# Weights in tiles of sixteen pairs, three sets of split parts, field 0 in an output slot: a bilinear pair kernel on one core

## The chip, the core and the metric

The kernel runs on one core of one Trainium2 chip. The metric is device time in microseconds. The core has five engines that run side by side and meet at semaphores: TensorE (PE; matrix products into PSUM), VectorE (DVE), ScalarE (ACT), GpSimd (POOL) and SyncE (SP), which here only issues DMAs. Sixteen DMA engines move data between the chip's main memory and the core's SBUF; SP, ACT and POOL each feed them from a queue of their own.

## The reference

There are 32 fields, each a batch of 1024 vectors of 128 numbers, and 496 pairs (i, j) of fields with i < j. Each pair has its own 128 x 128 matrix. For each pair the kernel multiplies the batch of field i by the matrix, and then, element by element, by field j:

```python
v_i = inputs[:, I_IDX, :]                              # (1024, 496, 128)
v_j = inputs[:, J_IDX, :]
transformed = jnp.einsum('bpd,ped->bpe', v_i, W)       # W: (496, 128, 128)
return transformed * v_j
```

All is float32. The output has 1024 x 496 x 128 numbers, 260 MB; the weights have 32.5 MB, the fields 16.8 MB.

## The kernel before

**Order.** Pairs are worked in the order i = 30, 29, ... 0, and for each i all j > i; a pair's number q is its place in this order. A field lies transposed, 128 x 1024. The main loop (L300) counts half pairs u: each step issues the first products of half u (`first`, L257) and the rest of half u - 3 (`second`, L273). The program fixes the order of the instructions on every engine; no planner moves them.

**Products.** The first 15 pairs are multiplied directly in float32 (L265). All others use TensorE's faster float32r format: weights and fields are each split in three parts, and a half pair is made of three 512-column matmuls: xh,wh and xl,wl (L268), then, after ACT has scaled PSUM in place (L270), xd,wd (L279). When both halves stand, one VectorE multiplication (L244) takes PSUM and field j and writes 128 x 1024 numbers into an output tile. PSUM holds four pairs.

**Splitting.** `split_w` (L144) splits a chunk of two pairs: ACT makes wh (L149), POOL makes wl (L151) and wd (L152, L153). There are four sets of these parts, so chunk c waits for the last use of chunk c - 4; its split is issued right behind that use. `split_x` (L161) splits half a field: ACT makes xh (L167), POOL makes xl (L168, L169), VectorE xd some steps later (L334). One split, of weights or of a field, is issued every second half step, the one that is needed soonest first.

**Weights.** Raw weights come in tiles of eight pairs: 128 rows of 4 KB, 62 loads of 512 KB, in three buffers. Loads up to tile 11 have places in the loop (`w_at`), later ones follow when the last split of an older tile has been issued (`ring`). Most are one DMA from SP (L132). The 25 loads in `WAPART` are divided (`load_apart`): POOL loads 112 rows over 14 of the 16 DMA engines, SP the last 16 rows, one on each engine. POOL's queue goes round the engines with a pointer; a tiny transfer (`move_on`, L111) puts the pointer back, so that the same two engines are left out each time. Field 0 comes late into one of the three weight buffers, in its turn in `ring`.

**Output.** The first 292 pairs are stored in groups of four, one DMA of 2 MB in 16 KB rows; the others in groups of three, 1.5 MB in 12 KB rows; ACT issues them (L318). A group's tile is four of the twelve slots of one buffer (`slots`), or one of the tiles g3, g2, g1, g0, which serve as output tiles until four fields each are loaded into them (the places in `XAT`, less `OWAIT`). From pair 292 on the twelve slots alone are used, four groups of three in turn. VectorE can write a slot only when the store that read it has landed.

Of the kernel before, what the change touches and what calls it, by code (L numbers as in the profile page):

```python
# [7 lines left out]
F32 = mybir.dt.float32  # L8
F32R = mybir.dt.float32r
ALU = mybir.AluOpType  # L10

P = 128
NF = 32
NQ = NF * (NF - 1) // 2
BT = 1024
HB = 512
WC = 2
WL = 8
OG = 4
EPS = 2.0**-12  # L20
NATIVE = 5
# [2 lines left out]
LAG = 3  # L24
SPREAD = 18
PB = 4
WB = 3
WLEAD = 12
XAFTER = 54
WRING = 12  # L30
XLEAD = 5

XG = 4
NE = 14
ROWS = 8 * NE
WAPART = tuple(range(12, 62, 2))
BACK = 3
FOURS = 73
NS = 12
XAT = (313, 219, 141, 52)  # L40
OWAIT = 20
XSTEP = 6
SLAG = 2
# [7 lines left out]

def _groups():

    return [(q, OG) for q in range(0, OG * FOURS, OG)] + [(q, OG - 1) for q in range(OG * FOURS, NQ, OG - 1)]


@with_exitstack
def kernel(
# [22 lines left out]
    nc = tc.nc  # L81
# [3 lines left out]
    xpool = ctx.enter_context(tc.tile_pool(name="x", bufs=1))  # L85
    spool = ctx.enter_context(tc.tile_pool(name="xs", bufs=2))
    rpool = ctx.enter_context(tc.tile_pool(name="wr", bufs=WB))
    wpool = ctx.enter_context(tc.tile_pool(name="ws", bufs=1))
# [5 lines left out]
    def load_x(f, pieces=1, eng=None):  # L94
        if f == 0:

            t = rpool.tile([P, WL, P], F32, tag="w", name="x_0").rearrange("p q e -> p (q e)")
        else:
            t = xpool.tile([P, BT], F32, tag=f"x{f}", name=f"x_{f}")
        s = BT // pieces  # L100
        for k in range(pieces):
            (eng or nc.sync).dma_start(out=t[:, k * s : (k + 1) * s], in_=xt[f, :, k * s : (k + 1) * s])
        x_sb[f] = t

    w_raw = {}
# [3 lines left out]
    def move_on(k):  # L109

        nc.gpsimd.dma_start(out=mark[: 2 * k], in_=xt[0, : 2 * k, :16].rearrange("(b a) n -> a b n", a=k))  # L111

    def load_apart(dst, src):
        nc.gpsimd.dma_start(out=dst[:ROWS], in_=src[:ROWS].rearrange("(b a) m n -> a b m n", a=NE))
        nc.sync.dma_start(out=dst[ROWS:], in_=src[ROWS:])
# [3 lines left out]
    def load_group(k, m):  # L119
        if m == XG - 1:  # L120
            group[k] = xpool.tile([P, XG, BT], F32, tag=f"g{k}", name=f"x_g{k}")
        f = XG * k + 1 + m
        x_sb[f] = group[k][:, m, :]
        nc.sync.dma_start(out=x_sb[f], in_=xt[f])

    def load_w(c, splits=(0, WL), eng=nc.sync):
        w_raw[c] = rpool.tile([P, WL, P], F32, tag="w", name=f"w_{c}")
        if c in WAPART:
            load_apart(w_raw[c], wt[c])
            return  # L130
        for a, b in zip(splits, splits[1:]):
            eng.dma_start(out=w_raw[c][:, a:b, :], in_=wt[c, :, a:b, :])  # L132

    scaled, taken, halved = {}, {}, {}

    def apart(inst, other, reason="the halves of a pair lie in two banks"):

        if other is not None:
            tc.declare_no_dep(inst.ins, other.ins, reason=reason)

    w_s, spent = {}, []
    w_t = [[wpool.tile([P, WC * P], F32R, tag=f"{t}{k}", name=f"{t}_{k}") for t in ("wh", "wl", "wd")] for k in range(4)]

    def split_w(c, u):  # L144

        k = c * WC % WL
        raw = w_raw[c * WC // WL][:, k : k + WC, :].rearrange("p q e -> p (q e)")
        h, l, d = w_t[c % 4]
        halved[c] = nc.scalar.mul(h, raw, 1.0 - 2.0**-13)  # L149
        apart(halved[c], halved.get(c - 4), "one engine writes both, in order")  # L150
        nc.gpsimd.tensor_tensor(l, raw, h.bitcast(F32), ALU.subtract)  # L151
        nc.gpsimd.tensor_scalar(d, h.bitcast(F32), EPS, 1.0, ALU.mult, ALU.mult)  # L152
        nc.gpsimd.tensor_tensor(d, l.bitcast(F32), d.bitcast(F32), ALU.subtract)  # L153
        w_s[c] = (h, l, d)
        if (c + 1) * WC % WL == 0:
            spent.append(c * WC // WL)

    x_s = {}
    later = []
# [1 line left out]
    def split_x(f, a, u):  # L161

        if a == 0:
            x_s[f] = [spool.tile([P, BT], F32R, tag=t, name=f"{t}_{f}") for t in ("xh", "xl", "xd")]
        s = slice(a, a + HB)
        h, l, d = [t[:, s] for t in x_s[f]]
        nc.scalar.mul(h, x_sb[f][:, s], 1.0 - 2.0**-13)  # L167
        nc.gpsimd.tensor_tensor(l, x_sb[f][:, s], h.bitcast(F32), ALU.subtract)  # L168
        nc.gpsimd.tensor_scalar(l, l.bitcast(F32), 1.0 / EPS, 1.0, ALU.mult, ALU.mult)  # L169
        if f == 0 and a > 0:  # L170
            spent.append("x")
        if f > NF - 2 - NATIVE - SHARED:
            later.append((min(u + XDLAG, 2 * first_q[f] + LAG - 1), d, h.bitcast(F32), l.bitcast(F32)))
        else:
            nc.gpsimd.tensor_tensor(d, h.bitcast(F32), l.bitcast(F32), ALU.subtract)

    nq0 = NATIVE * (NATIVE + 1) // 2
    c0 = nq0 // WC
# [2 lines left out]


    todo = []
    for c in range(c0, nchunk):
        todo.append(((c - 3) * WC + 1, max(c * WC, nq0), lambda u, c=c: split_w(c, u)))
    for i in range(NF - 2 - NATIVE, -1, -1):
        for a in range(0, BT, HB):
            at = first_q[i + 1] + 1 if i < NF - 3 - NATIVE else 2
            if 0 < i < SPREAD:
                at += (NF - 2 - i) * (2 + 3 * (a > 0)) // 10  # L190
            todo.append((at, first_q[i], lambda u, i=i, a=a: split_x(i, a, u)))
    todo.sort(key=lambda t: t[1])

    load_w(0, (0, 1, WL), nc.sync)
    load_x(NF - 2, pieces=2, eng=nc.scalar)
    load_x(NF - 1, pieces=2, eng=nc.scalar)
    load_x(NF - 3)
    load_x(NF - 4)
    load_w(1, eng=nc.sync)
    for f in range(NF - 5, NF - 4 - XLEAD, -1):  # L200
        load_x(f)
    load_w(2, eng=nc.sync)


    w_at = {}
    for c in range(WB, -(-NQ // WL)):
        free = (c - WB + 1) * WL if (c - WB) * WL < nq0 else 0
        if c < WRING:
            w_at[max(c * WL - 3 * WC + 1 - WLEAD, free)] = c

    back = []
    last = NQ // WL
    ring = [*range(WRING - WB, XAFTER + 1), "x", *range(XAFTER + 1, last)]

    ngroup = NF // XG // 2
    group_at = {q + XSTEP * (XG - 1 - m): (k, m) for k, q in enumerate(XAT) for m in range(XG)}
    assert all(q + 5 < first_q[XG * k + m + 2] for q, (k, m) in group_at.items())
    until = {f"g{k}": q - OWAIT for k, q in enumerate(XAT)}
    groups = _groups()
    group_of = {q + k: (g, k) for g, (q, n) in enumerate(groups) for k in range(n)}  # L220
    used = {t: n - 9 for n, t in enumerate(("s0", "s1", "s2", *sorted(until, reverse=True)))}

    slots = opool.tile([P, NS, BT], F32, tag="slots", name="slots")
    written = {}

    def out_tile(g):
        q, n = groups[g]
        if n < OG:
            a = (g - FOURS) * n % NS
        else:  # L230
            t = min((t for t in used if q + n <= until.get(t, NQ)), key=used.get)
            used[t] = g
            if t in until:
                return xpool.tile([P, OG, BT], F32, tag=t, name=f"ot_{g}"), None
            a = OG * int(t[1:])
        return slots[:, a : a + n, :], a
# [63 lines left out]
    for u in range(2 * NQ + LAG + SLAG):  # L300
        q = u // 2
        if u < 2 * NQ:
            i, j = pairs[q]
            if u % 2 == 0 and j == i + 1 and XG * ngroup < i - 2 - XLEAD:
                load_x(i - 2 - XLEAD)
            first(u)
            if u == 2 * nq0:
                move_on(5)
            if u % 2 == 0 and q in group_at:
                load_group(*group_at[q])  # L310
            if u % 2 == 1 and q in w_at:
                load_w(w_at[q])
            if u % 2 == 0 and q in back:
                move_on(16 - NE if max(w_raw) < WAPART[-1] else 13)
        if LAG <= u < 2 * NQ + LAG:
            second(u - LAG)
        while stores and stores[0][0] <= u - LAG:
            nc.scalar.dma_start(*stores.pop(0)[1:])  # L318
        if u % 2 == 1:
            ready = [t for t in todo if t[0] <= q]  # L320
            if ready:
                ready[0][2](u)
                todo.remove(ready[0])
        if ring[WB:] and ring[0] in spent:
            ring.pop(0)
            c = ring[WB - 1]
            if c == "x":
                load_x(0)
            else:
                load_w(c)  # L330
            if c in WAPART:
                back.append(q + BACK)
        while later and later[0][0] <= u:
            nc.vector.tensor_tensor(*later.pop(0)[1:], ALU.subtract)  # L334
# [32 lines left out]
```

## Time and profile before

| | |
|---|---|
| median of three runs | 748.13 us (743.98 to 750.29) |
| profiled execution | 741.81 us, span 739.9 us |
| moved by DMA | 310.02 MB, mean 419 GB/s |
| TensorE, ACT, VectorE, POOL busy | 703.9, 634.0, 637.3, 595.0 us |
| weight loads | SP: 36 of 512 KB, 26 of 64 KB, one of 448 KB; POOL: 25 of 448 KB |
| a store of 2 MB in `slots` | 16.5 us from issue to landing (median); of 1.5 MB 12.6 us |

A row of busy time by stage gives the stretch in microseconds, its length, then for PE, PEld (weight loads of TensorE), DVE, ACT and POOL the busy time with the number of instructions, then the granted TensorE clock (1.00 is full), the DMA engines' busy share and GB/s. A row of waits names the engine, tile and line that waited, then what ended the wait: total us, number, longest. A row of the timeline gives start, duration, engine, line, operation, and tiles as out<-in. In the summary, DMA digits are the busy share of 40 equal slices in tenths; a queue's row gives packets, MB and the share of the span of sixteen engines.

### The profile page before, as it was taken

The numbers are of one execution on the slowest core, as the hardware profiler recorded it, in microseconds if no ns is written. First come the engines' busy times: TensorE is split into PE (matmuls) and PEld (weight loads), VectorE is DVE, ScalarE is ACT, GpSimd is POOL, SyncE is SP. The second block draws the span as 40 slices with busy tenths as digits, with TensorE's granted clock in tenths as the row PEclk, the third lists the DMA queues.
The fourth block names the chain that finished last, engine by engine and source line by source line (L and its number), as shares of the span: only waits on it lengthen the run. The fifth ranks groups of instructions, "written<-read, shape, count | busy, mean of one in ns | idle before, by whom it ended". The sixth has DMA issues, their size and how long they took to land.

```text
span 739.9 us, 10346 instructions
## 1 busy us (share of the span) xinstructions
PE 703.9 (95%) x2946; PEld 550.4 (74%) x2946; DVE 637.3 (86%) x550; ACT 634.0 (86%) x1256; POOL 595.0 (80%) x882
## 2 busy tenths in 40 slices
PE   7999999999999999999899979999999999999994
PEld 3577777878778888776688758886778887777782
DVE  3898999999999999988798868987999988997884
ACT  1298999999999999998899968998989999898892
POOL 1789999999999999987789776988787888797660
PEclk9999999999999999999999999999999999999997
DMA  9999999999999999999999999999999999999998
GB/s 346 422 429 423 430 413 429 426 418 428 423 421 428 421 426 424 427 418 426 425 427 424 428 425 406 419 424 425 424 425 419 423 421 421 426 416 424 423 430 330
DMA packets 36968, 310.02 MB, mean 419 GB/s; under 512 B 5552, under 2 KB 5680, under 8 KB 19120
## 3 DMA queue, kind: packets, MB, share of 16 engines
q10 hardware_dynamic: 21888, 261.11, 83.6%
q1 hardware_dynamic: 10592, 36.77, 12.4%
q0 software_dynamic: 4432, 11.48, 4.0%
q8 instruction: 24, 0.39, 0.2%
q14 instruction: 32, 0.26, 0.1%
HBM read 49.29 MB, written 260.05 MB: 418 GB/s over the span
## 4 chain that ended last, share of the span: by engine, by line
PE 60%; DMA 22%; DVE 8%; POOL 3%; ACT 3%; issue 2%; ACTq 0%; DVEq 0%; POOLq 0%
PE po L268 38%; DMA out_dram<-slots 20%; PE po L279 18%; DVE slots L244 5%; PE po L265 4%; ACT po L270 2%; DVE xd L334 2%; DMA out_dram<-ot 1%; DVE ot L244 1%; POOL wd L153 1%; POOL wl L151 1%; POOL xl L168 1%; DMA x<-in_xt_dram 1%; POOL xl L169 0%; POOL wd L152 0%
## 5 line engine op out<-in xcount | busy, mean ns | idle before, releaser
L270 ACT ACTIVATE po<-po 128x512 f32<-128x512 f32 x962 | 553.3, 584 | 74.0 <-PE po L268 57.4
L268 PE MATMUL po<-xh,wh 128*128 128x512 f32 x962 | 382.0, 397 | 17.3 <-DVE slots L244 15.2
L279 PE MATMUL po<-xd,wd 128*128 128x512 f32 x962 | 376.4, 391 | 4.8 <-DVE xd L334 2.4
L268 PE MATMUL po<-xl,wl 128*128 128x512 f32 x962 | 377.2, 392 | 1.2 <-POOL wl L151 0.9
L244 DVE TENSOR_TENSOR slots<-po,x 128x1024 f32<-128x1024 f32 (+1 forms) x263 | 314.0, 1213 | 56.3 <-DMA out_dram<-slots 21.1
L268 PEld LDWEIGHTS po<-xh,wh 128*128 128x128 f32 x962 | 181.2, 188 | 74.0 <-DVE slots L244 30.8
L151 POOL TENSOR_TENSOR wl<-w,wh 128x256 fp32r<-128x256 f32 x241 | 184.8, 767 | 63.6 <-ACT wh L149 57.9
L279 PEld LDWEIGHTS po<-xd,wd 128*128 128x128 f32 x962 | 181.2, 188 | 45.0 <-DVE slots L244 3.2
L268 PEld LDWEIGHTS po<-xl,wl 128*128 128x128 f32 x962 | 181.3, 189 | 40.7 <-POOL wl L151 3.9
L153 POOL TENSOR_TENSOR wd<-wl,wd 128x256 fp32r<-128x256 f32 x241 | 180.3, 748 | 20.1
L244 DVE TENSOR_TENSOR slots<-po,x_g 128x1024 f32<-128x1024 f32 x123 | 148.4, 1223 | 22.3 <-DMA out_dram<-slots 8.5
L244 DVE TENSOR_TENSOR ot<-po,x 128x1024 f32<-128x1024 f32 x99 | 119.4, 1221 | 13.6 <-PE po L279 2.6
L152 POOL TENSOR_SCALAR wd<-wh 128x256 fp32r<-128x256 f32 x241 | 103.5, 429 | 20.5
L149 ACT ACTIVATE wh<-w 128x256 fp32r<-128x256 f32 x241 | 98.6, 410 | 5.7 <-DVE slots L244 5.7
L334 DVE TENSOR_TENSOR xd<-xh,xl 128x512 fp32r<-128x512 f32 x52 | 48.0, 924 | 0.0
L168 POOL TENSOR_TENSOR xl<-x_g,xh 128x512 fp32r<-128x512 f32 x32 | 41.6, 1300 | 2.2 <-ACT xh L167 2.0
L168 POOL TENSOR_TENSOR xl<-x,xh 128x512 fp32r<-128x512 f32 x20 | 25.8, 1292 | 15.8 <-ACT xh L167 15.6
L169 POOL TENSOR_SCALAR xl<-xl 128x512 fp32r<-128x512 f32 x52 | 34.4, 662 | 4.6
L265 PE MATMUL po<-x,w 128*128 128x512 f32 x60 | 29.5, 650 | 4.1 <-DMA x<-in_xt_dram 4.1
L265 PEld LDWEIGHTS po<-x,w 128*128 128x128 f32 x60 | 12.1, 207 | 20.7 <-issue 14.5
L167 ACT ACTIVATE xh<-x 128x512 fp32r<-128x512 f32 x20 | 12.3, 624 | 11.5 <-DMA x<-in_xt_dram 11.4
L167 ACT ACTIVATE xh<-x_g 128x512 fp32r<-128x512 f32 x32 | 20.0, 624 | 0.0
(8 smaller groups left out, 49.5 us busy)
## 6 DMA issues: line engine op xcount, KB each, us to landing
out_dram<-slots ACTq DMA_DIRECT2D x67, 1536.0 KB, 12.6
out_dram<-slots ACTq DMA_DIRECT2D x44, 2048.0 KB, 16.5
out_dram<-ot ACTq DMA_DIRECT2D x28, 2048.0 KB, 12.7
w<-in_wt_dram SPq DMA_DIRECT2D x36, 512.0 KB, 10.9
w<-in_wt_dram POOLq DMA_DIRECT2D x25, 448.0 KB, 11.6
x_g<-in_xt_dram SPq DMA_DIRECT2D x16, 512.0 KB, 16.3
x<-in_xt_dram SPq DMA_DIRECT2D x14, 512.0 KB, 9.4
out_dram<-slots ACTq DMA_DIRECT2D x5, 512.0 KB, 8.9
```

Source lines behind the costliest of these rows:

```text
L149: halved[c] = nc.scalar.mul(h, raw, 1.0 - 2.0**-13)
L151: nc.gpsimd.tensor_tensor(l, raw, h.bitcast(F32), ALU.subtract)
L152: nc.gpsimd.tensor_scalar(d, h.bitcast(F32), EPS, 1.0, ALU.mult, ALU.mult)
L153: nc.gpsimd.tensor_tensor(d, l.bitcast(F32), d.bitcast(F32), ALU.subtract)
L168: nc.gpsimd.tensor_tensor(l, x_sb[f][:, s], h.bitcast(F32), ALU.subtract)
L169: nc.gpsimd.tensor_scalar(l, l.bitcast(F32), 1.0 / EPS, 1.0, ALU.mult, ALU.mult)
L244: i = nc.vector.tensor_tensor(ot[:, k, s], p, f, ALU.mult)
L265: nc.tensor.matmul(po[q][:, s], w_raw[q // WL][:, q % WL, :], x_sb[i][:, s], start=True, stop=True)
L268: m = nc.tensor.matmul(po[q][:, s], w_s[c][t][:, r], x_s[i][t][:, s], start=t == 0, stop=t == 1)
L270: scaled[u] = nc.scalar.mul(po[q][:, s], po[q][:, s], 1.0 + EPS)
L279: m = nc.tensor.matmul(po[q][:, s], w_s[q // WC][2][:, r], x_s[i][2][:, s], start=False, stop=True, skip_group_check=True)
L334: nc.vector.tensor_tensor(*later.pop(0)[1:], ALU.subtract)
```

## The change

- Weight tiles hold sixteen pairs (`WL = 16`): rows of 8 KB, 31 loads of 1 MB, two buffers. The first tile comes in three pieces, the second whole before the loop. All later loads follow when the last split of the tile two before has been issued, none before pair 15.
- 13 of the 31 loads are divided over 14 engines and the rest (`WAPART`), every second one from tile 6 on, as before every second one from tile 12 of eight pairs.
- The fourth set of split weights lies in tile g0 and is used up to pair 178 only; after that there are three sets, and a split waits for the chunk three before. g0 becomes an output tile from pair 188 on.
- Field 0 is loaded at pair 432 into slot 11 of the output slots and split at pairs 444 and 448 (before: 436 and 437). For two rounds the last group has two pairs, so that slot 11 stays free.
- Fields of the four groups are loaded at pairs 308, 212, 117 and 52 (before: 313, 219, 141, 52).

```diff
-WL = 8
+WL = 16
-WB = 3
-WLEAD = 12
-XAFTER = 54
-WRING = 12
+WB = 2
+WSETS = 4
+WMORE = 178
+XZERO = 432
+XSPLIT = 444
+XROUND = 11
-WAPART = tuple(range(12, 62, 2))
+WAPART = tuple(range(6, 31, 2))
-XAT = (313, 219, 141, 52)
+XAT = (308, 212, 117, 52)
...
 def _groups():
-    return [(q, OG) for q in range(0, OG * FOURS, OG)] + [(q, OG - 1) for q in range(OG * FOURS, NQ, OG - 1)]
+    groups, q = [(q, OG) for q in range(0, OG * FOURS, OG)], OG * FOURS
+    while q < NQ:
+        k, n = divmod(len(groups) - FOURS, NS // (OG - 1))
+        n = OG - 1 - (n == NS // (OG - 1) - 1 and k - XROUND in (0, 1))
+        groups.append((q, min(n, NQ - q)))
+        q += n
+    return groups
...
         if f == 0:
-            t = rpool.tile([P, WL, P], F32, tag="w", name="x_0").rearrange("p q e -> p (q e)")
+            t = slots[:, NS - 1, :]
+            for h in (0, 1):
+                written.pop((NS - 1, h))
...
-    w_t = [[wpool.tile(...) for t in ("wh", "wl", "wd")] for k in range(4)]
+    w_t = [[wpool.tile(...) for t in ("wh", "wl", "wd")] for k in range(WSETS - 1)]
+    more = xpool.tile([P, OG * BT], F32R, tag="g0", name="w_more")
+    w_t.append([more[:, k * WC * P : (k + 1) * WC * P] for k in range(3)])
...
-        h, l, d = w_t[c % 4]
+        h, l, d = w_t[set_of[c]]
...
-        if (c + 1) * WC % WL == 0:
-            spent.append(c * WC // WL)
+        if (c + 1) * WC % WL == 0 and c * WC // WL + WB < NQ // WL:
+            ring.append(c * WC // WL + WB)
...
+    set_of, user, order = {}, {}, list(range(WSETS))
+    last_of = dict.fromkeys(order, c0 - WSETS)
     for c in range(c0, nchunk):
-        todo.append(((c - 3) * WC + 1, max(c * WC, nq0), lambda u, c=c: split_w(c, u)))
+        if c * WC == WMORE:
+            order.remove(WSETS - 1)
+        order.append(order.pop(0))
+        set_of[c] = order[-1]
+        user[c], last_of[order[-1]] = last_of[order[-1]], c
+        todo.append(((user[c] + 1) * WC + 1, max(c * WC, nq0), lambda u, c=c: split_w(c, u)))
...
             at = first_q[i + 1] + 1 if i < NF - 3 - NATIVE else 2
+            if i == 0:
+                at = XSPLIT + 4 * (a > 0)
...
-    load_w(0, (0, 1, WL), nc.sync)
+    load_w(0, (0, 1, WL // 2), nc.sync)
...
-    load_w(1, eng=nc.sync)
+    load_w(0, (WL // 2, WL), nc.sync)
     for f in range(NF - 5, NF - 4 - XLEAD, -1):
         load_x(f)
-    load_w(2, eng=nc.sync)
+    load_w(1)
...
-            t = min((t for t in used if q + n <= until.get(t, NQ)), key=used.get)
+            t = min((t for t in used if q + n <= until.get(t, NQ) and (t != "g0" or q >= WMORE + OWAIT // 2)), key=used.get)
...
-            if u % 2 == 1 and q in w_at:
-                load_w(w_at[q])
+            if u == 2 * XZERO:
+                load_x(0)
...
-        if ring[WB:] and ring[0] in spent:
-            ring.pop(0)
-            c = ring[WB - 1]
-            if c == "x":
-                load_x(0)
-            else:
-                load_w(c)
+        while ring and q >= nq0:
+            c = ring.pop(0)
+            load_w(c)
             if c in WAPART:
                 back.append(q + BACK)
```

More of the change, by code (lines that the diff above doesn't have):

```diff
@@ L126, in load_w @@
     def load_w(c, splits=(0, WL), eng=nc.sync):
-        w_raw[c] = rpool.tile([P, WL, P], F32, tag="w", name=f"w_{c}")
+        if c not in w_raw:
+            w_raw[c] = rpool.tile([P, WL, P], F32, tag="w", name=f"w_{c}")
         if c in WAPART:
@@ L139, in apart @@
             tc.declare_no_dep(inst.ins, other.ins, reason=reason)
-    w_s, spent = {}, []
-    w_t = [[wpool.tile([P, WC * P], F32R, tag=f"{t}{k}", name=f"{t}_{k}") for t in ("wh", "wl", "wd")] for k in range(4)]
+    w_s, ring = {}, []
+    w_t = [[wpool.tile([P, WC * P], F32R, tag=f"{t}{k}", name=f"{t}_{k}") for t in ("wh", "wl", "wd")] for k in range(WSETS - 1)]
+    more = xpool.tile([P, OG * BT], F32R, tag="g0", name="w_more")
+    w_t.append([more[:, k * WC * P : (k + 1) * WC * P] for k in range(3)])
     def split_w(c, u):
@@ L147, in split_w @@
         raw = w_raw[c * WC // WL][:, k : k + WC, :].rearrange("p q e -> p (q e)")
-        h, l, d = w_t[c % 4]
+        h, l, d = w_t[set_of[c]]
         halved[c] = nc.scalar.mul(h, raw, 1.0 - 2.0**-13)
-        apart(halved[c], halved.get(c - 4), "one engine writes both, in order")
+        apart(halved[c], halved.get(user[c]), "one engine writes both, in order")
         nc.gpsimd.tensor_tensor(l, raw, h.bitcast(F32), ALU.subtract)
@@ L169, in split_x @@
         nc.gpsimd.tensor_scalar(l, l.bitcast(F32), 1.0 / EPS, 1.0, ALU.mult, ALU.mult)
-        if f == 0 and a > 0:
-            spent.append("x")
         if f > NF - 2 - NATIVE - SHARED:
@@ L198 @@
     load_x(NF - 4)
-    load_w(1, eng=nc.sync)
+    load_w(0, (WL // 2, WL), nc.sync)
     for f in range(NF - 5, NF - 4 - XLEAD, -1):
         load_x(f)
-    load_w(2, eng=nc.sync)
[L205 to L209, printed above, removed]
+    load_w(1)
     back = []
-    last = NQ // WL
-    ring = [*range(WRING - WB, XAFTER + 1), "x", *range(XAFTER + 1, last)]
     ngroup = NF // XG // 2
@@ L219 @@
     groups = _groups()
+    assert groups[-1][0] + groups[-1][1] == NQ
     group_of = {q + k: (g, k) for g, (q, n) in enumerate(groups) for k in range(n)}
@@ L228, in out_tile @@
         if n < OG:
-            a = (g - FOURS) * n % NS
+            a = (g - FOURS) % (NS // (OG - 1)) * (OG - 1)
         else:
-            t = min((t for t in used if q + n <= until.get(t, NQ)), key=used.get)
+            t = min((t for t in used if q + n <= until.get(t, NQ) and (t != "g0" or q >= WMORE + OWAIT // 2)), key=used.get)
             used[t] = g
```

## The prediction

> **What bounds the kernel now.** I read the summary first, then the DMA queues, then busy time by stage, then the waits, and last single rows of the timeline. The page's engine line and its DMA lines:
>
> ```profile
> PE 703.9 (95%) x2946; PEld 550.4 (74%) x2946; DVE 637.3 (86%) x550; ACT 634.0 (86%) x1256; POOL 595.0 (80%) x882
> ...
> DMA  9999999999999999999999999999999999999998
> ...
> q10 hardware_dynamic: 21888, 261.11, 83.6%
> q1 hardware_dynamic: 10592, 36.77, 12.4%
> q0 software_dynamic: 4432, 11.48, 4.0%
> ```
>
> TensorE is at 95%, but the three queues' packets fill 83.6 + 12.4 + 4.0 = 100% of sixteen engines' span. q10 is ACT's stores (12 and 16 KB rows), q1 is SP's loads, q0 is POOL's. By stage:
>
> ```profile
> 110.00:280.00 170.00, 168.77 (x730) 135.49 (x729) 157.72 (x138) 159.68 (x319) 156.63 (x229) 1.00 1.01 424
> 280.00:440.00 160.00, 151.47 (x649) 120.01 (x648) 134.09 (x117) 142.58 (x282) 134.98 (x203) 1.00 1.01 424
> 540.00:620.00 80.00, 78.72 (x343) 63.52 (x342) 72.33 (x63) 73.91 (x148) 67.43 (x103) 1.00 1.01 422
> 620.00:700.00 80.00, 77.73 (x336) 61.99 (x334) 68.70 (x60) 72.37 (x143) 62.68 (x97) 1.00 1.01 422
> ```
>
> The last two columns (DMA share, GB/s) stand at 1.01 and 422 to 424 in every stage. The waits from 540 to 700 us agree: apart from POOL's harmless wait for ACT, the largest is VectorE waiting for stores to free a slot, and TensorE then waiting for VectorE.
>
> ```profile
> DVE slots L244 <- DMA out_dram<-slots: 9.7, 15, 1.9
> ...
> PEld po L268 <- DVE slots L244: 8.7, 14, 1.5
> ```
>
> So **DMA throughput is the bound**, with TensorE close behind. How close: undisturbed, a half pair starts every 0.68 us (weight loads of xh,wh at 613.85, 614.53, 615.21, 615.89), 1.36 us a pair. The first weight load of pair 178 stands at 266.0 us, of pair 330 at 490.6, of pair 380 at 563.8, of pair 495 at 725.7. TensorE's spare time to pair 495 is therefore 459.7 - 317 x 1.36 = 28.6 us from pair 178, 235.1 - 165 x 1.36 = 10.7 us from 330, and 161.9 - 115 x 1.36 = 5.5 us from 380. At the very end the last store, 256 KB, is issued at 732.4 and lands at 738.9, 6.4 us later; the first x load of that size took 2.7 us. So 3.7 us at the end are still DMA backlog, not TensorE.
>
> **The change, part by part.** (1) *8 KB rows.* Median packets in the trace: 4 KB 159 ns, 12 KB 460 ns, 16 KB 611 ns. The line through 4 and 16 KB is 36.8 ns per KB above 4 KB, so 8 KB is 159 + 151 = 310 ns against 2 x 159 = 318. Thirty loads x 128 rows = 3,840 merged rows x 8.3 ns / 16 engines = 2.0 us. Each DMA also ends with about sixteen 4-byte packets of 9 ns; 30 SP loads, 12 POOL loads and 12 pointer moves fewer: 54 x 16 x 9 / 16 = 0.5 us. Sum **-2.5 us**. The only 8 KB packets in the trace, 38 instruction fetches, have a median of 309. No load or store row of 8 KB was timed, so both ends: nothing, if a row still travels as two 4 KB packets; at most q10's rate for all weights: q10 takes 618.6 us / 261.11 MB = 2.37 us/MB, q1 2.50, q0 2.58, so 21.0 MB x 0.13 + 11.5 MB x 0.21 = -5.0 us. I take the line, since 12 KB lies on it (159 + 301 = 460). Nothing hides this gain: these engines are the bound.
>
> The Trainium skill (DMA: Bandwidth & Descriptors, "Anatomy of one DMA") puts a fixed 2.0 us on every DMA. By it, 42 fewer loads would save 84 us as an estimate. The rows above speak against reading it so: at a share of 1.01 that latency lies under other transfers, and only packet time counts.
>
> (2) *13 instead of 25 loads over 14 engines.* An engine that is left out carries one row of each such load instead of nine: relieved by 25 x 8 x 4 KB = 800 KB before and 13 x 8 x 8 KB = 832 KB after; the balance stays. POOL issues 12 loads (624 ns) and 12 pointer moves (637 ns) fewer, 15 us of its 595; POOL isn't the bound, so nothing.
>
> (3) *Three sets of parts from pair 178.* This is the cost. A split's issue moves two pairs later (2.72 us) in ACT's and POOL's order, to just behind the use of the set three chunks back. Without field work the parts are ready early enough:
>
> ```profile
> 691.51 0.41 ACT L149 ACTIVATE wh<-w 128x256 fp32r<-128x256 f32 x1
> 692.00 0.74 POOL L151 TENSOR_TENSOR wl<-w,wh 128x256 fp32r<-128x256 f32 x1 [0.67 <-ACT wh L149]
> ...
> 696.43 0.19 PEld L268 LDWEIGHTS po<-xl,wl 128*128 128x128 f32 x1
> ```
>
> wl ends at 692.74, TensorE loads it at 696.43: 3.69 us, less 2.72 leaves 0.97. Where a half of a field's split stands before it on POOL, it doesn't:
>
> ```profile
> 611.50 1.30 POOL L168 TENSOR_TENSOR xl<-x_g,xh 128x512 fp32r<-128x512 f32 x1
> 612.90 0.61 POOL L169 TENSOR_SCALAR xl<-xl 128x512 fp32r<-128x512 f32 x1
> 613.59 0.74 POOL L151 TENSOR_TENSOR wl<-w,wh 128x256 fp32r<-128x256 f32 x1
> ```
>
> That wl ends at 614.33 and its weight load is at 616.12: 1.79 us, less 2.72 is a **stall of 0.93 us**. Behind the stalled load wait the chunk's other matmuls, then ACT's L270 and VectorE's product. The next chunk had 3.16, so the stall doesn't run on. The other late halves leave 1.67 to 2.33 us, so 0.4 to 1.05 a half. Halves of a field issued from pair 178 on: 23; from 330: 10; from 380: 6. At 0.93: 21.4 us against 28.6 spare, 9.3 against 10.7, 5.6 against 5.5. TensorE ends about where it does now; the spare time was waiting for slots. Value 0; ends: 0 and, if every half cost the full 2.72, 62.6 - 28.6 - 3.7 = +30 us.
>
> (4) *Fewer output tiles early.* g0 holds parts until pair 178 and g2 goes to fields 24 pairs sooner, so 4 tiles remain from pair 97 (before: from 199). With 4 tiles a tile comes back 16 pairs later: from its store's issue to its next write some 12 x 1.40 - 0.3 = 16.5 us. Stores between 115 and 228 us land in 10.8 to 13.5 us. So 0; where fields load beside them (up to 17 us) VectorE waits, but with three stores in flight the engines stay full. 280 to 440 us shows that case: four tiles, share 1.01.
>
> (5) *Loads in SP's order.* At the start field rows 19 and 18 pass ahead of a weight load that waited, and the second tile is 1 MB: 512 KB more before it lands, 1.5 us at the first slice's 346 GB/s, so 19.3 instead of 17.8 us, while ACT comes to those weights at 23.9. Later one 1 MB load has 16 pairs (22 us) instead of two of 512 KB sharing them; 512 KB land in 8 to 20 us now, and a row of twice the size takes a larger turn beside the store's rows. 0; if one is late, a few us once, out of TensorE's spare 28.6.
>
> (6) *Field 0 in slot 11.* Its load, issued at pair 432 (636 us), waits on SP for the store of pairs 421 to 423, issued at 628.6 and landed at 641.6; field 0 took 9.8 us, so it is there at 651.4, and ACT wants it at pair 444, about 653.5. The next weight load behind it on SP comes at pair 443. 2 us to spare; if late, ACT's evictions queue behind, a few us against 3 + 3.7 spare. In rounds 11 and 12 eleven slots instead of twelve: backlog stays near 11 us. 0.
>
> **Sum.** 741.81 us for the profiled execution (span 739.9) - 2.5 = 739.3. It lay below the runs shown; carried to their median, 748.13 - 2.5 = **745.6**.
>
> **Rivals.** *Late parts decide* (slower). With 28.6 us spare and 3.7 at the end, 23 halves turn to a loss from 32.3 / 23 = 1.40 us a half; the mechanism is POOL's field work standing before L151's subtraction with no set in hand. At 1.9 us, twice my value, 43.7 - 32.3 = +11.4: 759.5. For: between 150 and 232 us four sets already leave 0.05 us at the worst chunks, and POOL L151 held weight loads for 3.9 us in 110 to 280. Against: after 250 us halves stand 6 to 9 pairs apart, and POOL has 0.77 us free in each 2.72. *Rows aren't merged*: packets stay 4 KB, only the 0.5 us remains: 747.6. *A larger gain*: the handover at pair 292 idles TensorE for 5.4 us, and the granted clock is 0.57 from 440 to 448. With another tile order that falls away, and 5.0 us come from the rows: 743; over 1% takes luck of the runs too, 740.
>
> The skill (TensorE: Matmul & The Clock Gate, "What's actually happening") halves the clock after about 3.4 us idle; the handover agrees, and a 0.93 us stall shouldn't trigger it.
>
> **Chances.** Forecast 0.62 (743 to 748), unmerged 0.12, late parts 0.20 (0.16 of it over 1%), larger gain 0.06. 1%, 7.5 us, is about what a measurement of this kernel can tell from no change; the runs before span 744.0 to 750.3. The range: down to 741.5 (-5.0 with 1.5 of scatter), up to 756 (1.74 us a half: 40.0 - 32.3 = +7.7). Faster by over 1%: 0.06; within: 0.76; slower: 0.18, two points of it from field 0 or the first loads.
>
> **What would show it.** Right: DMA share still 1.01, q1 and q0 together near 16.1% (now 16.4) with some 4,500 packets fewer, TensorE's waits for POOL L164 (the old L151) some 15 to 25 us in 178 to 495, those for slots smaller by as much, last landing near 736. Wrong: a DMA share below 1.00 after 300 us, stalls on L164 over 1.4 us each, ACT waiting for field 0 near 654 us.

## The result and the profile after

| | before | after |
|---|---|---|
| median of 20 runs each, side by side | 748.50 us (741.72 to 752.52) | 746.66 us (744.95 to 749.8) |
| ratio after / before | | 0.999, 95% interval 0.9968 to 1.0012 |
| profiled execution, its span | 741.81, 739.9 us | 749.8, 748.0 us |
| packets of all DMAs | 36,968 | 31,880 |

Side by side the change makes no difference that can be measured: 745.6 us were forecast, 746.66 came out. A second comparison (third experiment) gave 1.0036, so between 2.4 us faster and 4.5 us slower all is open. In the comparisons of this document the median of the kernel before lies between 743.96 and 748.50 us, that of the kernel after at 746.66 and 747.11. The two pages exaggerate: the profiled execution of the kernel after was its slowest, that of the kernel before one of its fastest. What can be compared are shares, packets and single rows, not the spans.

First the summary of the kernel after: busy time of the engines, DMA share in 40 slices, and the queues with packets, MB and share.

```profile
PE 707.9 (95%) x2946; PEld 553.0 (74%) x2946; DVE 638.2 (85%) x550; ACT 635.0 (85%) x1256; POOL 579.2 (77%) x858
...
DMA  9999999999999999999999999999999999999998
...
q10 hardware_dynamic: 21888, 261.11, 82.9%
q1 hardware_dynamic: 7616, 36.31, 12.6%
q0 software_dynamic: 2320, 11.94, 4.1%
```

The same picture as before: 99.6% of sixteen engines' span is packets. But read the last two lines against those of before. The loads (q1 and q0) have 5,088 packets fewer and should have taken 2.5 us less; they take 16.7% of 748.0 = 124.9 us, where they took 16.4% of 739.9 = 121.3 us. **The part that was to become shorter became longer in this profile.**

By stage (stretch, length, busy time of PE, PEld, DVE, ACT, POOL with instruction numbers, granted clock, DMA share, GB/s), kernel after:

```profile
110.00:280.00 170.00, 167.42 (x718) 134.46 (x717) 155.36 (x136) 157.22 (x314) 150.54 (x219) 0.99 1.01 425
280.00:440.00 160.00, 155.40 (x664) 122.92 (x663) 139.73 (x121) 145.17 (x287) 128.43 (x194) 1.00 1.01 423
540.00:620.00 80.00, 78.81 (x341) 63.35 (x341) 71.52 (x61) 73.89 (x148) 64.48 (x99) 1.00 1.01 419
620.00:700.00 80.00, 74.60 (x316) 59.94 (x315) 66.48 (x57) 67.59 (x135) 58.50 (x90) 0.98 0.98 394
640.00:680.00 40.00, 34.71 (x142) 27.36 (x141) 30.07 (x25) 30.63 (x61) 26.95 (x41) 0.96 0.96 372
```

Up to 440 us the DMA share and the rate are as before. From 540 to 620 the share still reads 1.01, at 419 GB/s instead of 422. Between 640 and 680 us there is a real hole: share 0.96, where the kernel before had

```profile
640.00:680.00 40.00, 38.68 (x168) 30.94 (x167) 34.52 (x31) 36.16 (x72) 33.18 (x52) 1.00 1.01 421
```

It is a place where TensorE waits for VectorE and VectorE for stores, which shows in the waits from 540 to 700 us (who waited, for what: total us, times, longest):

```profile
DVE slots L257 <- DMA out_dram<-slots: 7.9, 6, 4.1
PEld po L281 <- DVE slots L257: 7.6, 5, 3.9
...
PEld po L281 <- POOL wl L164: 3.5, 6, 1.2
```

The third line is the new wait, of the three sets of parts. One of them in the timeline, first POOL, then TensorE's weight load (start, duration, engine, line, operation, in brackets the idle time before and its end):

```profile
616.58 1.30 POOL L181 TENSOR_TENSOR xl<-x_g,xh 128x512 fp32r<-128x512 f32 x1
617.96 0.62 POOL L182 TENSOR_SCALAR xl<-xl 128x512 fp32r<-128x512 f32 x1
618.67 0.74 POOL L164 TENSOR_TENSOR wl<-w,wh 128x256 fp32r<-128x256 f32 x1
```

```profile
619.46 0.19 PEld L281 LDWEIGHTS po<-xl,wl 128*128 128x128 f32 x1 [0.49 <-POOL wl L164]
```

A half field stands before the subtraction, wl ends at 619.41, and the weight load follows at once, having waited for 0.49 us: the mechanism of step (3), at half its size.

### The profile page after: what moved, and what is told of

The parts are those of the page before. It is cut to its first block, busy times and chain, and to the rows that moved or that the text cites. A ratio compares the mean times of both kernels' runs of the same rounds, so it can differ in the third digit from the quotient of the medians.

```text
span 748.0 us, 10230 instructions
## 1 busy us (share of the span) xinstructions
PE 707.9 (95%) x2946; PEld 553.0 (74%) x2946; DVE 638.2 (85%) x550; ACT 635.0 (85%) x1256; POOL 579.2 (77%) x858
## 2 busy tenths in 40 slices
DMA packets 31880, 310.01 MB, mean 414 GB/s; under 512 B 4304, under 2 KB 4432, under 8 KB 10064
## 4 chain that ended last, share of the span: by engine, by line
PE 60%; DMA 19%; DVE 9%; ACT 5%; POOL 3%; issue 2%; ACTq 0%; DVEq 0%; POOLq 0%
PE po L281 38%; PE po L292 18%; DMA out_dram<-slots 16%; DVE slots L257 5%; ACT po L283 4%; PE po L278 4%; DMA out_dram<-ot 3%; DVE xd L343 2%; DVE ot L257 2%; POOL wl L164 1%; DMA x<-in_xt_dram 1%; POOL xl L181 1%; POOL wd L166 0%; ACT wh L162 0%; ACTq L331 0%
## 5 line engine op out<-in xcount | busy, mean ns | idle before, releaser
L257 DVE TENSOR_TENSOR slots<-po,x 128x1024 f32<-128x1024 f32 (+1 forms) x282 | 337.8, 1214 | 50.3 <-DMA x<-in_xt_dram 10.9
L281 PE MATMUL po<-xh,wh 128*128 128x512 f32 x882 | 350.1, 397 | 18.7 <-DVE slots L257 17.0
L281 PE MATMUL po<-xl,wl 128*128 128x512 f32 x882 | 347.2, 394 | 2.2 <-POOL wl L164 1.5
L292 PE MATMUL po<-xd,wd 128*128 128x512 f32 x882 | 346.0, 392 | 2.4 <-DVE slots L257 2.4
L281 PEld LDWEIGHTS po<-xh,wh 128*128 128x128 f32 x882 | 166.5, 189 | 67.8 <-DVE slots L257 28.6
L257 DVE TENSOR_TENSOR slots<-po,x_g 128x1024 f32<-128x1024 f32 x128 | 155.0, 1223 | 36.7 <-DMA out_dram<-slots 15.6
L166 POOL TENSOR_TENSOR wd<-wl,wd 128x256 fp32r<-128x256 f32 x221 | 163.2, 738 | 18.4
L257 DVE TENSOR_TENSOR ot<-po,x 128x1024 f32<-128x1024 f32 x80 | 96.6, 1221 | 14.6 <-PE po L292 6.1
L181 POOL TENSOR_TENSOR xl<-x,xh 128x512 fp32r<-128x512 f32 x18 | 23.2, 1288 | 16.1 <-ACT xh L180 15.8
L281 PE MATMUL po<-xh,w_more 128*128 128x512 f32 x80 | 32.4, 406 | 2.3 <-DVE ot L257 2.2
L292 PE MATMUL po<-xd,w_more 128*128 128x512 f32 x80 | 31.4, 393 | 2.4 <-DVE xd L343 2.4
L281 PE MATMUL po<-xl,w_more 128*128 128x512 f32 x80 | 32.1, 401 | 0.1
```

The costliest lines, as they stand in the source:

```text
L257: i = nc.vector.tensor_tensor(ot[:, k, s], p, f, ALU.mult)
L281: m = nc.tensor.matmul(po[q][:, s], w_s[c][t][:, r], x_s[i][t][:, s], start=t == 0, stop=t == 1)
L292: m = nc.tensor.matmul(po[q][:, s], w_s[q // WC][2][:, r], x_s[i][2][:, s], start=False, stop=True, skip_group_check=True)
```

## The experiments

The theory after the first look: the shorter rows gain what was worked out, and the late sets, or the slot of field 0, give it back beside a DMA share that hides it. The rivals: the rows gain nothing, or the loads in their new form cost as much as they save. Two measures are used. One is the time against the kernel before, run on the same chip. The other is the time of the load packets in the profiled execution: in the third column (share of q1 + share of q0) x span, which the page's rounding leaves uncertain by some 0.7 us; in the fourth, from the trace's packets, by how much they exceeded the medians of their sizes (sum / 16 engines; the medians are those of the kernel before, 309 ns for 8 KB). To kernels that leave out field 0, which SP loads, 1.3 us are added back in the third column (128 packets of 4 KB x 161.5 ns mean / 16 engines). Field 31 comes by ACT's queue, which this column doesn't count, so nothing is added where it is left out.

| kernel | time / before, 95% interval | load packets, us | over medians, us |
|---|---|---|---|
| before, first profile | | 121.3 | 2.3 |
| before, again | 0.9999 (0.9968 to 1.0030) | 121.5 | 3.3 |
| after, first profile | 0.9990 (0.9968 to 1.0012) | 124.9 | 8.8 |
| after, again | 1.0036 (1.0013 to 1.0060) | 122.7 | 6.5 |
| after, 17 loads in 4 KB rows | 1.0015 (0.9992 to 1.0038) | 124.4 | 7.3 |
| before, three late sets | 1.0058 (1.0024 to 1.0093) | 125.2 | 6.7 |
| after without field 0 in a slot | 1.0000 (0.9974 to 1.0025) | 122.3 + 1.3 | 7.6 |
| after without field 31 | 1.0003 (0.9975 to 1.0031) | 125.4 | 9.1 |
| the same, four sets | 0.9992 (0.9966 to 1.0018) | 122.8 | 7.1 |
| after, late fields in quarters | 1.0038 (1.0014 to 1.0062) | 125.4 | 9.4 |
| the same, on POOL alone | 1.0028 (1.0008 to 1.0049) | 124.5 | 9.0 |
| after, tiles of sixteen pairs alone | 0.9982 (0.9950 to 1.0014) | 121.7 + 1.3 | 6.9 |

**1. Rows of 4 KB in the loads of 1 MB.** Same loads, same order; the halves of a tile lie apart in memory.

```diff
...
+        half = wt[c].rearrange("p m n -> (p m n)").rearrange("(h p x) -> p h x", h=2, p=P)
+        if splits == (0, WL):
+            eng.dma_start(out=w_raw[c].rearrange("p (h m) n -> p h (m n)", h=2), in_=half)
+            return
...
-            eng.dma_start(out=w_raw[c][:, a:b, :], in_=wt[c, :, a:b, :])
...
```

> The changed kernel, but the 17 undivided loads of 1 MB travel as 4 KB rows: the rows lie in two halves in main memory, everything else, the number of DMAs too, is as in the changed kernel. If packet time is what counts and the line through the medians holds (8.3 ns a merged row): 17 x 128 x 8.3 / 16 = 1.1 us slower than the changed kernel. If 8 KB rows bring long packets with them (SP's 8 KB packets had a mean of 344 ns beside their median of 309 in the one profile, 5.2 us in all): 2 to 4 us faster than the changed kernel, with a mean near 162 ns for the 4 KB packets.

746.1 us against 747.11 of the kernel after on the same chip: 1.0 us less, not more, and within what the intervals allow. Whatever 8 KB rows save, the time doesn't show it. The load packets exceeded their medians by 7.3 us with 4 KB rows too (SP's 4 KB packets had a mean of 167.6 ns beside 159), so what lengthens them isn't the size of a row alone.

**2. The kernel before with three late sets.** Nothing else of the change.

```diff
+WMORE = 178
...
-        h, l, d = w_t[c % 4]
+        h, l, d = w_t[set_of[c]]
...
+        if c * WC == WMORE:
+            order.remove(3)
+        order.append(order.pop(0))
+        set_of[c] = order[-1]
...
-        todo.append(((c - 3) * WC + 1, max(c * WC, nq0), lambda u, c=c: split_w(c, u)))
+        todo.append(((user[c] + 1) * WC + 1, max(c * WC, nq0), lambda u, c=c: split_w(c, u)))
```

> The kernel before with one part of the change: three sets of split parts from pair 178, the fourth lies idle. If DMA is the bound and TensorE's stalls are hidden: time within 2 us of the kernel before, weight loads of xl,wl waiting for POOL at each late half of a field, 0.4 to 1.05 us each, 10 to 24 us in all from pair 178 on, and the waits for slots smaller by as much. If late parts decide: 5 us or more slower, the DMA share under 1.00 after 300 us.

750.42 against 745.68 us; by the ratio 4.3 us slower (1.8 to 6.9). On the kernel before the late sets aren't free. The waits of the whole run:

```profile
PEld po L276 <- POOL wl L152: 14.6, 23, 2.4
PE po L276 <- POOL wl L152: 5.0, 6, 2.0
```

The two rows don't add up: each wait of the matmuls (PE) lies inside one of the weight loads' waits (PEld). TensorE thus stood for 14.6 us, of which 10.5 after 266 us. The longest wait, 2.4 us, ends at 661.6 us; from 200 to 620 us none is over 1.3. POOL splits the halves of field 0 there at 653.69 and 658.44 us (pairs 436 and 437 in the program's order), which the change spreads to pairs 444 and 448; so this kernel's late sets are not quite those of the changed kernel. The stages of this kernel show the same sign as those of the kernel after, a nearly full share with fewer GB/s:

```profile
540.00:620.00 80.00, 77.06 (x330) 60.75 (x329) 67.50 (x59) 71.86 (x142) 63.74 (x98) 1.00 1.00 409
620.00:700.00 80.00, 76.70 (x330) 60.83 (x328) 68.86 (x59) 71.15 (x141) 63.61 (x98) 1.00 1.00 404
```

**3. The kernel after, again**, on that chip, as the measure for the others.

> The changed kernel unchanged, for a second profile and as the yardstick of the other three. Theory: 1 to 3 us faster than the kernel before; a profile nearer the median than the first one (749.8 us) has the gap of TensorE at pair 438 (5.2 us) again, if it comes from the eleven slots, and not, if it came from slow loads in that execution.

747.11 us, 1.0036 of the kernel before (2.7 us slower, 1.0 to 4.5). The hole came at the same place: pair 438 took 4.84 us instead of 1.36 (5.23 in the first profile, 1.5 or less before).

**4. Without field 0 in a slot.** Field 1 stands for it; all late groups have three pairs.

```diff
-        n = OG - 1 - (n == NS // (OG - 1) - 1 and k - XROUND in (0, 1))
+        n = OG - 1
...
-                load_x(0)
+                x_sb[0] = x_sb[1]
```

> The changed kernel without field 0's place: field 1 is used in its stead, nothing is loaded into slot 11 and all late groups have three pairs; left out is the load of 512 KB, and the output of field 0's pairs is that of field 1. If DMA throughput alone counts: 512 KB less at 424 GB/s, 1.2 us faster than the changed kernel. If the eleven slots of rounds 11 and 12 starve the DMA engines (share 0.963 from 640 to 680 us in the first profile, 1.5 us): 2.5 to 4 us faster, and no wait over 3 us for slots between pairs 430 and 450.

745.15 us, 2.0 less than the kernel after, of which 1.3 are the load itself. Pair 438 is down to less than 1.5 us, and 640 to 680 us move more:

```profile
640.00:680.00 40.00, 38.22 (x164) 30.33 (x163) 34.97 (x31) 35.40 (x71) 30.86 (x47) 1.00 1.01 405
```

(396 GB/s in the kernel after on the same chip.) So the hole belongs to the slot. What it costs beyond the load, 0.7 us by the medians, isn't resolved.

**5 and 6. Three sets and four, with the rest of the change.** In both, field 30 stands for field 31 (the first two lines); the second has four sets throughout in the place that this frees (all lines).

```diff
-    load_x(NF - 1, pieces=2, eng=nc.scalar)
+    x_sb[NF - 1] = x_sb[NF - 2]
...
-    ... for k in range(WSETS - 1)]
-    more = xpool.tile([P, OG * BT], F32R, tag="g0", name="w_more")
+    ... for k in range(WSETS)]
...
-        if c * WC == WMORE:
-            order.remove(WSETS - 1)
```

> The changed kernel with field 30 in the place of field 31: left out is the load of field 31 at the start (512 KB), and the output of field 31's pairs is that of field 30. It frees 4 KB per partition and is the yardstick of the next one. About 1 us faster than the changed kernel (512 KB at 424 GB/s), the late halves' stalls on the subtraction of wl as there: 0.97 us to spare without field work, 0.05 with it.

> The same without field 31, but the freed place holds the fourth set of split parts to the end; nothing else differs from e5. If the late parts cost what the kernel before lost to them alone (4.3 us): 3 to 5 us faster than e5, no wait of weight loads for POOL after pair 178, and less time of long load packets after 480 us. If they are hidden, as predicted: within 1.5 us of e5.

746.94 and 745.27 us: 1.7 us for the fourth set, between the two expectations and not resolved (the intervals overlap). The waits of TensorE for POOL's wl after 275 us went from 9.1 us (weight loads) to none that the list shows.

**7 and 8. Half of the weights, with four sets and with three.** Both are the kernel before, load only four of a tile's eight matrices and use each for two pairs; this is to leave TensorE as the bound.

```diff
-    def load_w(c, splits=(0, WL), eng=nc.sync):
+    def load_w(c, splits=(0, WL // 2), eng=nc.sync):
...
-        k = c * WC % WL
+        k = c * WC % (WL // 2)
```

> The kernel before with half of each weight tile loaded and used twice (left out: 16 MB of weight loads; half of the pairs are multiplied by another pair's matrix). Packet time falls by about 37 us (4 KB rows become 2 KB rows, 159 to 84 ns), so if DMA throughput is the bound with TensorE close behind, TensorE takes over: 712 to 725 us, the DMA share under 0.99, few waits for slots.

> The same with three sets of parts from pair 178 on. With the DMA cover gone, the 23 late halves show in full: at 0.93 us each 21 us slower than e7, at the least 8 us if VectorE's and ACT's lag after a half covers part of each stall. If the stalls are not what costs: within 3 us of e7.

718.87 and 729.56 us. With 38.1 us of packets less (732.1 to 694.0 at medians) the kernel before became 28 us faster, TensorE's spare time from pair 178 on fell from 28.6 to 5.4 us, and the late sets then cost 10.7 us (their intervals, 0.959 to 0.9673 and 0.9748 to 0.9838, don't touch), between the 8 and the 21 that were expected. The DMA share, expected under 0.99, still read 0.99 to 1.01 in the stages from 110 to 700 us. TensorE waited for wl in the second:

```profile
PEld po L276 <- POOL wl L152: 21.0, 30, 2.4
PE po L276 <- POOL wl L152: 8.1, 11, 2.0
```

Here too the second row lies inside the first. Of the 21.0 us, 16.9 come after 266 us, where the kernel with four sets has none: they cost 10.7 where little covers them. In the kernel before, 10.5 us of such waits went with 4.3. The price of a wait thus isn't its length; that it is set by what else waits at the time is the reading that fits, not one that was tested alone.

**9. The kernel before, again.**

> The kernel before, unchanged, profiled a second time. Its first profile (741.8 us) was among the shortest of its runs; there the packets of all queues took 10.1 us more than at their medians (sum over 16 engines), in all profiles of kernels with three late sets 15.4 to 18.1 us. If the long packets come with the late sets, this profile has again about 10 us of them, and waits for POOL from pair 178 below 2 us. If they are a matter of the execution, it has 14 to 18 us and a span of 744 to 749 us. Time 1.000 of the kernel before, within 0.3%.

744.31 us, ratio 0.9999, with a span of 745.7 us in the profile, 5.8 more than in the first. Its queues:

```profile
q10 hardware_dynamic: 21888, 261.11, 83.2%
q1 hardware_dynamic: 10592, 36.77, 12.3%
q0 software_dynamic: 4432, 11.48, 4.0%
```

The load packets took the same to 1 us, in an execution 5.8 us longer. All packets together exceed their medians by 12.7 us, against 10.1 in the first profile and 15.3 to 18.1 in all kernels with all weights and with the tiles of sixteen pairs or the late sets: between the two expectations, and the span is as the second expected. So a part of the long packets is a matter of the execution. Waits for POOL after 266 us aren't in its list. What the changed kernels add is in the loads: 6.5 to 9.4 us over the medians, against 2.3 and 3.3.

**10 and 11. Late fields in quarters.** A quarter of a field's split before wl costs POOL 1.3 us instead of 2.1.

```diff
+XFINE = 11
...
-    def split_x(f, a, u):
+    def split_x(f, a, u, w=HB):
-        s = slice(a, a + HB)
+        s = slice(a, a + w)
...
-        for a in range(0, BT, HB):
+        w = HB // 2 if i < XFINE else HB
+        for a in range(0, BT, w):
```

> The changed kernel with its late fields (0 to 10) split in quarters of 256 columns, on ScalarE and POOL, in place of halves; nothing else. A quarter costs POOL about 1.2 us (a half 2.0), against 0.97 us of room a weight chunk, so the shortage is 0.2 to 0.6 us instead of 0.93 and the next chunks make it good. If the late stalls are what costs the changed kernel its gain, the waits of TensorE for POOL's weight parts after pair 178 fall from 10 us to under 3 and the time falls by 1 to 4 us against the changed kernel (743 to 745.5 where that is at 746.7). If the stalls lie beside the transfers and cost nothing, the waits fall as much and the time stays within 1 us. ScalarE gets 23 more operations of about 0.3 us fixed cost.

> As the kernel with quarters, but ScalarE still rounds halves; only POOL's low parts of fields 0 to 10 go in quarters. Separates POOL's share from ScalarE's: if POOL's half is what stalls TensorE, waits and time as with quarters on both, within 1 us; if ScalarE's own half field in front of the high parts matters, waits stay above 4 us and the gain is less than half.

747.47 and 746.5 us. TensorE's waits for wl from 275 to 735 us, which took 8.8 us in the kernel after (weight loads; the matmuls' 1.5 us lie inside), are in the kernel with quarters

```profile
PEld po L289 <- POOL wl L165: 3.8, 9, 0.6
...
PEld po L289 <- POOL xl L183: 1.6, 1, 1.6
...
PE po L289 <- POOL wl L165: 0.4, 2, 0.2
```

and 2.8 us with quarters on POOL alone. The one wait for xl is new in both, at 316 us, where a quarter of a field comes late. With it 8.8 us became 5.4 and 4.4, and the ratios, 1.0038 and 1.0028, are no better than those of the kernel after, 0.9990 and 1.0036. **In the changed kernel the late stalls cost nothing that shows.** These intervals, and the 1.7 us of the fifth and sixth kernels, still leave room for a cost of 3 to 4 us. As the waits for wl fell as far with ScalarE's halves kept, POOL's half field in front of wl is what made them. On ScalarE two quarters take 0.82 us where a half takes 0.62: 0.2 us more for each of 22 halves, not the 0.3 that was expected.

**12. The tiles of sixteen pairs alone**: four sets throughout and no late field 0, the edits of the fourth and the sixth kernel together.

```diff
-        n = OG - 1 - (n == NS // (OG - 1) - 1 and k - XROUND in (0, 1))
+        n = OG - 1
...
-                load_x(0)
+                x_sb[0] = x_sb[1]
...
-    load_x(NF - 1, pieces=2, eng=nc.scalar)
+    x_sb[NF - 1] = x_sb[NF - 2]
...
-        if c * WC == WMORE:
-            order.remove(WSETS - 1)
```

> The changed kernel without its other parts: four sets throughout (field 30 stands for 31, as its place is taken) and no late field 0 (field 1 stands for it, every late group has three pairs). What remains is the weight tiles of sixteen pairs, 13 divided loads, and the output tiles and load order that go with them. Two fields are not loaded: 2.5 us of packets less; with the 2.9 us less of the changed kernel the packets take 726.6 us at their medians, against 732.1 before. If the late sets and the slot gave the gain back, the long packets are again some 10 to 13 us as in the kernel before, and the time is 0.990 to 0.994 of the kernel before. If the loads of 1 MB themselves bring the long packets, they stay at 15 to 18 us, SP's part of them at 5 us or more (1.7 and 1.9 in the two profiles of the kernel before), and the time is 0.996 to 1.000.

0.9982 (0.9950 to 1.0014): 1.3 us faster, with two loads left out. With those back, if each is worth its 1.3 us of packets, tiles of sixteen pairs and what goes with them (loads divided, load order, output tiles) are worth between 1.1 us faster and 3.6 us slower; the 2.5 us that were forecast lie outside. No hole at pair 438, no wait for wl after 275 us, and still the load packets took 121.7 + 1.3 = 123.0 us, no less than the 121.3 and 121.5 of the kernel before; SP's alone are 5.2 us over their medians (1.7 and 1.9 in the kernel before). It shows already from 60 to 110 us, long before any late set. The rows of that stage, first the kernel before, then the kernel with the tiles alone:

```profile
60.00:110.00 50.00, 47.12 (x199) 36.37 (x198) 47.25 (x41) 45.15 (x91) 46.06 (x64) 1.00 1.01 423
```

```profile
60.00:110.00 50.00, 47.21 (x199) 36.36 (x198) 47.25 (x42) 45.08 (x91) 46.14 (x63) 1.00 1.01 408
```

The five engines do the same work in both, the DMA share is 1.01 in both, and one moves 423 GB/s, the other 408. In this stretch the packets of SP's loads of 1 MB issued at 78.0 and 101.4 us took 416 and 456 ns in the mean, where the median of all is 309; those of the load before them, from 55.7 us on, took 311. So not every load of 1 MB is lengthened.

No version that loads all fields and all weights was faster than both kernels.

## Why the prediction was right, point by point

The time (745.6 against 746.66) and the verdict, no change that can be told, were right; of the steps one failed, and its error was small enough not to matter. That the two times lie so close is luck in part: the 2.5 us that were taken off aren't there, and the median from which they were taken moves by more than that between comparisons (743.96 to 748.50 us).

**(1) 8 KB rows, -2.5 us: the failed term.** Rows do travel as 8 KB packets, their median is 309 ns as the line said (its slope of 36.8 ns holds for 1000 bytes; it is 37.7 for a KB of 1024), and the sum at medians fell by 2.9 us (732.1 to 729.2). But the sum was made of medians, and engines are occupied by means. The 4 KB packets of before had a mean of 162 ns beside their median of 159; the 8 KB packets after have 344 on SP and 331 on POOL beside 309 (332 and 326 in the second profile). The second profile of the kernel before has means of 162 on SP and 167 on POOL. Two old packets thus took 323 to 324 ns on SP and one new one 332 to 344, so there the gain of 8 ns became a loss of 8 to 21; on POOL, with 325 to 334 against 326 to 331, it lies between a gain of 8 and a loss of 6. In us: loads 121.3 and 121.5 before, 124.9 and 122.7 after, where 118.8 were forecast. The twelfth kernel bounds it by time, together with terms (2), (4) and (5), which it also has. The lower end that the prediction gave, nothing, wasn't low enough: a loss wasn't considered.

**(2) Divided loads, 0: right.** POOL's busy time fell by 15.8 us (595.0 to 579.2), 15 were worked out; POOL wasn't the bound, and the time doesn't show it. Stores took 2.37 to 2.38 us/MB as before.

**(3) Three sets, valued at 0 with an end at +30.** The stall is where it was worked out and smaller: 16 waits after 266 us, 8.8 us in all, so 0.55 a wait where 0.93 stood; the longest was 1.2, and none ran on into the next chunk. 15 to 25 us in all were forecast. Value 0 fits the changed kernel: taking about half of the waits away (quarters) or all of them (four sets) moved the time by no more than the intervals. It doesn't hold on the kernel before (+4.3 us) nor with half of the weights (+10.7 us, where 21.4 us of stalls stood in the prediction and 16.9 were measured). The cover named, TensorE's spare time, fits the dearest case: 28.6 us had become 5.4. But on the kernel before, the same cover was there and 4.3 us came through; the load packets took 3.9 us more over their medians there (6.7, against a mean of 2.8), though that they are how it came through isn't shown. Late sets alone and tiles alone (4.1) each lengthen the load packets by some 4 us; both together, in the kernel after, by 3.7 and 6.0. It isn't their sum, and what the late sets add there can't be told from the scatter.

**(4) Fewer output tiles, 0: nothing seen against it.** The case named, VectorE waiting while fields load, occurred: pair 147 took 3.90 us instead of 1.36, and 110 to 280 us still has a share of 1.01 and 425 GB/s. The twelfth kernel has the same gap (4.58 us), so its time can't tell this term from (1).

**(5) SP's order, 0: right.** Pair 15, the first in the fast format, began at 33.33 us, before at 32.95.

**(6) Field 0 in the slot, 0: the load was right, its neighbourhood not.** The load was issued at 648.25 us and landed at 657.16; ACT came to it at 666.5, so it wasn't late. But the backlog didn't stay near 11 us: the stores issued at 638.66 and 642.38, beside a 1 MB load, took 16.0 and 16.6 us, and TensorE stood at pair 438. In the first profile that is the one stage with a share below 1.00, which the prediction had named as a sign of error (in the second the share there is 1.00, at 396 GB/s). Its price, 0.7 us by medians, is unresolved.

Of the rivals, *rows aren't merged* falls by the 8 KB packets, though its time (747.6) is as near as the forecast's, and *a larger gain* falls with (1). *Late parts decide* turned at 1.40 us a half; the longest stall of any late half was 1.2.

The granted clock behaved as the row of before suggested. In the first profile it fell to half after the three long gaps (at 225.9, 454.6 and 656.0 us, behind pairs 147, 303 and 438, for 3.4, 6.8 and 3.4 us), in the second after the last two only, and in both after none of the stalls of up to 1.2 us. The Trainium skill (DMA: Bandwidth & Descriptors, "Anatomy of one DMA"), read as 2.0 us for each of 42 loads, would have made 84 us of it. The section describes the DMAs that POOL issues, and 12 of the 42 were POOL's; for these alone it would be 24 us, an estimate as well. No more than 2.4 us can be there by the measured ratio, so the trace's reading was the right one.

What stays open: why load packets become long. They do so with tiles of 1 MB in rows of 8 and of 4 KB, and with the late sets on loads of 512 KB, so neither the row nor the tile alone is the cause; and the second profile of the kernel before has more of them than the first. The runs show only what stands beside them (last section). Whether the true difference is a gain of 2 us or a loss of 4 can't be told either: 0.9990 and 1.0036 are both measured.

## What to carry to other kernels

Where transfers are the bound, add up what the packets took (queue share x span), not a median times a number: the price of a packet isn't fixed when the order and size of the loads change. Give a change that "only saves packets" an end below nothing. And price a stall twice, with its cover and without it: here three late sets cost nothing that shows in one kernel, 4.3 us in another and 10.7 in a third.

## What the runs showed of the hardware

A busy share of 1.01 doesn't mean full throughput. It counts a packet as long as it is under way, and single load packets took over six times their median (2,065 ns for one of 309, in the second profile of the kernel after). From 20 us on, the two profiles of the kernel before have 63 and 99 load packets of 4 or 8 KB of over 1.5 times their median, those of the kernel after 279 and 173, the late sets alone 244, the tiles alone 221, the tiles in 4 KB rows 263. In these seven profiles 4.2 to 7.4 of the sixteen engines were moving a store's packet, in the mean, in the middle of such a packet; at the other load packets 9.3 to 10.5 were. Long load packets thus go with moments when stores run short. As 15.6 to 16.2 packets were under way in both cases, these are also the moments when many load packets run side by side, and the two can't be told apart here.

Few stores alone aren't enough. From 3 to 15 us, before the output starts, 0.1 to 2.0 engines were moving packets of 2 KB or more from ACT's queue, sixteen packets were under way, and the 4 KB load packets, most of them of fields, took 161 to 163 ns in the mean. In the first profile of the kernel after the long packets are those of weights: its 4 KB load packets, all but one load of them of fields, have a mean of 161.6 ns, its 8 KB load packets, all of weights, 339; with at most four engines at stores as they began (from 20 us on) the means are 178 and 434. All this is read from the packets and not tested by itself.
